# Layer 0 of a four-layer network: scans of 1024 tokens by channel halves, with the neighbouring images' stages in bands between them

## The chip, the cores and the metric

One core of one Trainium2 chip runs the whole kernel in one launch. The metric is the device time of a run in microseconds (us); a kernel's time is the median of its runs. The engines are named as in the profile: PE (TensorE), PEld (its weight loads), DVE (VectorE), ACT (ScalarE), POOL (GpSimd), SP (the queue that issues the DMAs).

## The reference, cut to what matters

The network has four layers over four images of 64 x 64 tokens and 128 features. Only layer 0 is touched. Its inside, cut:

```python
xz = x @ in_proj_w.T;  xh, z = split(xz, 2);  z = silu(z)      # 256 channels each
xc = silu(depthwise_conv3x3(xh) + conv_b)
xs = 4 directions of xc: by rows, by columns, and both reversed # K = 4
x_dbl = einsum('bkdl,kcd->bkcl', xs, x_proj_weight)             # 8 + 16 + 16 rows
delta = softplus(dt_projs(x_dbl[:8]) + bias)
A = -exp(A_logs)                                                # 16 states
# for each token:  h = exp(delta*A) * h + (delta*u) * B ;  y = sum_n h_n * C_n
y = ys + Ds * xs, summed over the four directions
y = layer_norm(y) * out_norm_w + out_norm_b;  y = y * z
return y @ out_proj_w.T                                         # then x + this (not shown)
# ... a group norm of x stands in front of it; layers 1 to 3 left out
```

The recurrence in h is what costs: 4 images x 4 directions x 4096 tokens x 256 channels x 16 states.

## The kernel before: the parts that are touched

A step is one direction `k` and one chunk `c` of 512 tokens, both channel halves.

```python
tmp = pool("l0tmp", 2);  ps = pool("l0ps", 2, space=PSUM);  psy = pool("l0psy", 1, space=PSUM)
for b in range(NB):
    # ... conv stage of image b, all of it: group norm, in_proj, 9 conv products a chunk,
    #     Silu into xc (whole image in SBUF), z to DRAM; all PE products in tag "m"

    def inputs(k, c):
        xd_ps = ps.tile([40, CH], F32, name="xd_ps", tag="m")
        # ... two products; ACT copies them to xd; rows 8:24 (B) go to DRAM
        for s in range(2):
            dp = ps.tile([P, CH], F32, name="dp", tag="m")
            nc.tensor.matmul(dp, lhsT=w_dt[...], rhs=xd[0:8, :], start=True, stop=True)
            nc.scalar.activation(delta[:, s, :], dp, AF.Softplus, bias=dt_b[:, k, s : s + 1])
        # ... POOL: du = delta * u

    for i, (k, c) in enumerate(steps):
        for g in range(4):                     # four states at a time
            Bb = tmp.tile([P, 4, CH], F32, name="Bb", bufs=3)     # B, broadcast by DMA
            h = big.tile([P, 2, CH, 4], F32, name="h", tag="h", bufs=2)
            for q in range(4):
                n = 4 * g + q
                dB = tmp.tile([P, 2, CH], F32, name="dB", bufs=3)
                nc.gpsimd.tensor_tensor(dB, du, Bb[:, q : q + 1, :].to_broadcast([P, 2, CH]), ALU.mult)
                for s in range(2):
                    dA = ps.tile([P, CH], F32, name="dA")
                    nc.scalar.activation(dA, delta[:, s, :], AF.Exp, scale=A_neg[:, k, s, n : n + 1])
                    nc.vector.tensor_tensor_scan(
                        h[:, s, :, q], dA, dB[:, s, :], state[:, s, n : n + 1], ALU.mult, ALU.add)
            # ... state saved; at g == 0: ready = inputs(next step)
            cr = ps.tile([P, CH], F32, name="cr", tag="m")        # C, spread for the products
            nc.tensor.matmul(cr, lhsT=sel[:, g, :], rhs=xd, start=True, stop=True)
            nc.vector.tensor_tensor(W, cr..., diag..., ALU.mult)
            for q in range(4):
                for e in range(2):
                    pt = ps.tile([P, 2, 2, P], F32, name="pt")
                    # ... four transposes of h into pt; ACT copies pt to hT (4 buffers)
                # ... four products yT += W * hT
        # ... y = yT (+ the earlier direction's y), stored; statistics of y at k == 2
    # ... norm/gate/out_proj stage of image b, all of it
```

## Time and profile before

| | before |
|---|---|
| median time | 10,989.8 us (4 runs, 10,984.5 to 11,016.0) |
| profiled span | 10,995.2 us, mean granted PE clock 0.910 of full |
| layer 0 ends near | 7,820 us |
| two steps (1024 tokens, both halves) | 98 to 107 us by direction |

The prediction below shows the slices, the stretches, the chain and the groups. Two more views are needed to compare with. The waits, as "engine line waited for: us in total, times, longest us":

```profile
POOL dB L242 <- DVE h L246: 1006.4, 829, 5.9
...
DVE h L246 <- POOL dB L242: 699.8, 10, 174.3
DVE h L246 <- ACT dA L245: 627.2, 924, 2.8
```

The 699.8 us are ten long waits, mostly the serial stages between images. Second, the stretch of the last direction of image 3 (start:end, length, busy and instructions of PE, PEld, DVE, ACT and POOL, then the granted clock, the DMA share and GB/s):

```profile
7312.26:7721.74 409.48, 356.35 (x2274) 174.00 (x2272) 344.00 (x352) 323.27 (x537) 306.85 (x156) 0.99 0.27 94
```

That is four times 1024 tokens, 102.4 us each, with PE at 87% and its clock at 0.99.

### The profile page before, as it was taken

To read this page: it belongs to the slowest core of one execution; us is meant where nothing else is said; L and a number is where in the kernel's file an instruction comes from. 1 tells how busy PE (TensorE), PEld (TensorE's weight loads), DVE (VectorE), ACT (ScalarE), POOL (GpSimd) and SP (SyncE) were. 2 spreads that over 40 slices of the span, in tenths; PEclk is the share of its full clock that TensorE was granted. 3 is DMA by queue.
4 is the path that set the end of the run, shared out by engine and by line. 5 is a ranking of instruction groups with operands and counts; after the bars stand their busy time and mean duration, and the time that the engine had idled before them with its cause. 6 is when DMAs were issued, how large, how long until landed. Compare 5 with 4: busy or idle time off the path is not lost.

```text
span 10995.2 us, 136237 instructions
## 1 busy us (share of the span) xinstructions
PE 9042.7 (82%) x48616; PEld 4817.3 (44%) x48616; DVE 7870.9 (72%) x11236; ACT 6496.6 (59%) x11794; POOL 5549.4 (50%) x3106
## 2 busy tenths in 40 slices
PE   8888887888888888888887888888797666576777
PEld 4433444443344344334444333444575334344555
DVE  2788887277888717788881778888445876877777
ACT  3778876377888727778871778887222102114555
POOL 2777877277788727778872777887200000000000
PEclk9999999889999988999998899999898667678999
DMA  2223322222233222223322222332300011010000
GB/s 71 86 98 105 108 101 92 74 86 94 101 110 106 86 79 87 95 99 110 105 91 69 97 95 102 107 108 95 106 16 22 20 31 31 0 31 7 9 9 9
DMA packets 375737, 811.01 MB, mean 74 GB/s; under 512 B 24546, under 2 KB 289506, under 8 KB 309266
## 3 DMA queue, kind: packets, MB, share of 16 engines
q1 hardware_dynamic: 372946, 799.82, 21.7%
q8 instruction: 385, 6.31, 0.2%
q14 instruction: 294, 2.41, 0.1%
q10 hardware_dynamic: 2112, 2.48, 0.1%
HBM read 680.58 MB, written 121.63 MB: 73 GB/s over the span
## 4 chain that ended last, share of the span: by engine, by line
PE 61%; DVE 21%; ACT 10%; issue 4%; DMA 2%; POOL 2%; ACTq 0%; DVEq 0%; SPq 0%; POOLq 0%
PE yT L277 15%; PE pt L269 14%; DVE h L246 10%; ACT hT L271 6%; PE cr L254 5%; PE cv L163 5%; PE pm L776 2%; PE xd_ps L193 2%; PE po L923 2%; ACT dA L245 2%; PE dp L201 2%; PE ps L891 1%; DVE W L256 1%; PE po L441 1%; PE pf L436 1%
## 5 line engine op out<-in xcount | busy, mean ns | idle before, releaser
L246 DVE TENSOR_TENSOR_SCAN h<-dA,state,dB 128x512 f32<-128x512 f32 x4096 | 5016.9, 1271 | 1398.9 <-POOL dB L242 699.8
L242 POOL TENSOR_TENSOR dB<-du,Bb 128x1024 f32<-128x1024 f32 x2048 | 4842.1, 2370 | 1267.6 <-DVE h L246 1006.4
L245 ACT ACTIVATE dA<-delta,A_neg 128x512 f32<-128x512 f32 x4096 | 2788.5, 696 | 527.8 <-DVE h L246 514.3
L269 PE MATMUL pt<-ident,h 128*128 128x128 f32 x16384 | 2667.0, 292 | 348.4 <-DVE h L246 348.1
L269 PEld LDWEIGHTS pt<-ident,h 128*128 128x128 f32 x16384 | 1838.6, 145 | 2000.1 <-issue 1280.2
L271 ACT COPY hT<-pt 128x512 f32<-128x512 f32 x4096 | 2252.5, 587 | 748.9 <-PE pt L269 737.8
L277 PE MATMUL yT<-hT,W 128*32 128x256 f32 x16384 | 2324.7, 403 | 355.5 <-ACT hT L271 353.2
L277 PEld LDWEIGHTS yT<-hT,W 128*32 128x32 f32 x16384 | 540.0, 109 | 1440.3 <-ACT hT L271 1019.9
L696 POOL COPY XG<-Xs 64x1 f32<-64x1 f32 x4 | 0.7, 180 | 1784.9 <-ACT Xs L667 1784.9
L204 POOL TENSOR_TENSOR du<-delta,xc 128x1024 f32<-128x1024 f32 x128 | 335.0, 2617 | 763.2 <-ACT delta L202 763.2
L254 PE MATMUL cr<-xd,sel 40*128 40x512 f32 x1024 | 624.6, 715 | 49.4 <-ACT delta L202 36.3
L256 DVE TENSOR_TENSOR W<-cr,diag 128x512 f32<-128x512 f32 x512 | 351.1, 686 | 395.4 <-PE cr L254 264.1
L163 PE MATMUL cv<-pad,taps 128*128 128x512 f32 x1152 | 496.2, 592 | 0.0
L883 POOL COPY vw<-pad 128x196 f32<-128x196 f32 x256 | 76.5, 350 | 702.6 <-PE pv L915 590.7
L193 PE MATMUL xd_ps<-xc,w_x 128*40 128x512 f32 x512 | 354.3, 817 | 93.4 <-DVE W L256 91.1
L776 PE MATMUL pm<-PT,Xs 64*128 64x512 f32 x512 | 380.3, 919 | 16.3 <-DVE pr L777 16.3
L163 PEld LDWEIGHTS cv<-pad,taps 128*128 128x128 f32 x1152 | 216.9, 189 | 278.0 <-issue 274.4
L170 ACT ACTIVATE xc<-cv,cols 128x512 f32<-128x512 f32 x64 | 44.0, 687 | 446.6 <-PE cv L163 446.6
L923 PE MATMUL po<-PT,V 98*128 98x256 f32 x1024 | 278.4, 394 | 35.6 <-DVE PT L919 35.6
L628 ACT COPY S<-pa 128x512 f32<-128x512 f32 x96 | 56.2, 585 | 420.6 <-PE pa L621 420.6
L201 PE MATMUL dp<-xd,w_dt 8*128 8x512 f32 x512 | 291.4, 653 | 6.1 <-ACT xd L195 6.1
L581 PE MATMUL in_pm<-in_mv,tok 128*128 128x32 f32 x48 | 14.1, 386 | 324.4 <-DVE in_mv L579 324.4
(268 smaller groups left out, 9455.2 us busy)
## 6 DMA issues: line engine op xcount, KB each, us to landing
Bb<-l_B SPq DMA_DIRECT2D x512, 1024.0 KB, 4.7
l_y<-y SPq DMA_DIRECT2D x128, 512.0 KB, 3.1
yr<-l_y SPq DMA_DIRECT2D x64, 512.0 KB, 4.8
l_z<-z SPq DMA_DIRECT2D x32, 512.0 KB, 2.9
zf<-l_z SPq DMA_DIRECT2D x32, 512.0 KB, 3.9
yr<-l_y SPq DMA_DIRECT2D x64, 256.0 KB, 4.9
yf<-l_y SPq DMA_DIRECT2D x32, 512.0 KB, 4.7
xt<-in_x SPq DMA_DIRECT2D x32, 256.0 KB, 3.0
```

The costliest lines, as they stand in the source:

```text
L163: nc.tensor.matmul(pm, lhsT=taps[:, s, t, :], rhs=pad[:, 8 * c + dy : 8 * c + dy + 8, dx : dx + 64], start=(t == 0), stop=(t == 8),)
L193: nc.tensor.matmul(xd_ps, lhsT=w_x[:, s, k, :], rhs=u[:, s], start=(s == 0), stop=(s == 1))
L201: nc.tensor.matmul(dp, lhsT=w_dt[:, k, s * P : (s + 1) * P], rhs=xd[0:8, :], start=True, stop=True)
L242: nc.gpsimd.tensor_tensor(dB, du, Bb[:, q : q + 1, :].to_broadcast([P, 2, CH]), ALU.mult)
L245: nc.scalar.activation(dA, delta[:, s, :], AF.Exp, scale=A_neg[:, k, s, n : n + 1])
L246: nc.vector.tensor_tensor_scan(h[:, s, :, q], dA, dB[:, s, :], state[:, s, n : n + 1], ALU.mult, ALU.add)
L254: nc.tensor.matmul(cr, lhsT=sel[:, g, :], rhs=xd, start=True, stop=True)
L269: nc.tensor.transpose(pt[:, r, s, :], h[:, s, t0 : t0 + 32, :].rearrange("p t n -> p (t n)"), sh.ident)
L271: nc.scalar.copy(hT, pt.rearrange("p r s d -> p r (s d)"))
L277: nc.tensor.matmul(yT[e][32 * jo : 32 * jo + 32, qo % 2, :], lhsT=W[:, 4 * q + j, :], rhs=hTs[j // 2][:, j % 2, :], start=((e, jo) not in ...
L776: nc.tensor.matmul(pm, lhsT=Xs[:, r, :], rhs=PT[:, 8 * g : 8 * g + 8, :], start=True, stop=True)
L923: nc.tensor.matmul(po[:, e], lhsT=V[:, half, :], rhs=PT[:, half].rearrange("p h q -> p (h q)"), start=(half == 0), stop=(half == 1),)
```

## The change

The intent: pay a scan's fixed cost (some 0.2 us) half as often, let PE make one `hT` per product in place of two, and hide the serial conv and norm stages of the neighbouring images between scans. A unit is now 1024 tokens of one channel half `s`; two units are a pair, the work of two old steps. `before(b+1)` and `after(b-1)` are generators whose pieces ("bands") are emitted at g == 2 and g == 1. The diff, cut to its core:

```diff
+    L = 2 * CH                                   # 1024 tokens; NQ = 8
-            # conv stage of the whole image (xn, xc in SBUF, tag "m")
+        def before(b):                           # 8 statistics pieces, then 8 x (pad piece, conv piece)
+            ...
+                    pm = ps.tile([P, CH], F32, name="cv", tag="pt")      # was tag "m"
+                    ...                                                   # 9 products
+                    xo = tmp.tile([P, CH], F32, name="xo", tag="t2", bufs=4)
+                    nc.scalar.activation(xo, pm, AF.Silu, bias=conv_b[:, s : s + 1])
+                    nc.sync.dma_start(scr(f"xr{b % 2}")[s, :, c * CH : (c + 1) * CH], xo)
+                    xw = tmp.tile([P, 64, 8], F32, name="xw", tag="t2", bufs=4)
+                    nc.vector.tensor_copy(xw, xo.rearrange("p (h w) -> p w h", w=64))
+                    nc.sync.dma_start(scr(f"xw{b % 2}")...[:, :, 8 * c : 8 * c + 8], xw)   # pieces of 32 B
+                    zp = ps.tile([P, CH], F32, name="zp", tag="pt")
+                    ...                                                   # Silu to z, z to DRAM
+        def after(b, st):                        # 8 norm/gate/out_proj bands, one POOL product each
+        def fetch(b, k, c):                      # u of the next pair, from xr or xw in DRAM
         def inputs(k, c, u):
-                    dp = ps.tile([P, CH], F32, name="dp", tag="m")        # 2 a step
+                    dp = ps.tile([P, CH], F32, name="dp", tag="pt")       # 4 a pair
-                Bb [P, 4, CH] bufs=3;  dB [P, 2, CH] bufs=3;  h [P, 2, CH, 4] bufs=2;  W, 2 bufs
+                Bb [P, 2, L] bufs=2;   dB [P, L] bufs=2;      h [P, L, 4] bufs=2;      W, 5 bufs
-                            dA = ps.tile([P, CH], F32, name="dA")         # 2 buffers, 2 banks
+                    dA = ps.tile([P, L], F32, name="dA")                  # 2 buffers, 4 banks
+                    nc.scalar.activation(dA, delta[:, s, :], AF.Exp, scale=A_neg[:, k, s, n : n + 1])
+                    nc.vector.tensor_tensor_scan(h[:, :, q], dA, dB, state[:, s, n : n + 1], ALU.mult, ALU.add)
-                    cr = ps.tile([P, CH], F32, name="cr", tag="m")
+                        cr = ps.tile([P, CH], F32, name="cr", tag="pt")   # 2 a group, at s == 0 only
+                if g == 1: next(post, None)      # a norm band
+                if g == 2: next(pre, None)       # a statistics, pad or conv piece
```

## The prediction

> **What bounds the kernel now.** I read the busy table and the 40 slices first, then stretches of one image, then the chain of waits, the groups, and the DMA list.
>
> The page's slices, from the span's start to its end (tenths busy):
> ```profile
> PE   8888887888888888888887888888797666576777
> DVE  2788887277888717788881778888445876877777
> ACT  3778876377888727778871778887222102114555
> POOL 2777877277788727778872777887200000000000
> ```
> The POOL line shows layer 0: four identical images, about 29 slices, the last layer-0 work ending near 7820 us of 10995 us. The rest is layers 1 to 3, which the change does not touch. Four dips of DVE and POOL are the serial stages between the scans. The stretches of image 0 (window, length, then busy and instruction count of PE, PEld, DVE, ACT, POOL, the granted clock, DMA share, GB/s):
> ```profile
> 188.00:1877.00 1689.00, 1472.23 (x8829) 687.12 (x8828) 1377.84 (x1265) 1345.25 (x2226) 1308.06 (x668) 0.95 0.28 99
> 1877.00:1962.00 85.00, 42.86 (x204) 37.09 (x204) 31.27 (x42) 10.54 (x18) 56.26 (x24) 0.67 0.46 137
> 1962.00:2136.00 174.00, 162.26 (x411) 75.91 (x410) 7.84 (x13) 34.56 (x56) 0.00 (x0) 0.95 0.10 33
> ```
> Scans take 1689 us, the norm/gate/out_proj stage 85 us, the next image's conv stage 174 us: a period of about 1957 us. In the scan stage four engines are 77 to 87% busy; none is saturated. The chain of waits over that stage says who leads:
> ```profile
> by line: PE yT L277 24.6%; PE pt L269 23.7%; DVE h L246 15.6%; ACT hT L271 9.6%; PE cr L254 8.0%; issue 4.0%; PE xd_ps L193 3.0%; ACT dA L245 2.9%; PE dp L201 2.9%; DVE W L256 1.8%; DVE y L300 0.7%; ACT delta L202 0.6%; ACT L202 0.5%; DMA B
> ```
> PE leads (transposes, products, cr, xd, dp), through the alternation transpose, copy, product. A timeline piece of PE in direction 0 (start, duration, idle before):
> ```profile
> 1120.02 0.64 PE L277 MATMUL yT<-hT,W 128*32 128x256 f32 x8
> 1120.59 1.09 PE L269 MATMUL pt<-ident,h 128*128 128x128 f32 x8
> 1121.97 0.41 PE L277 MATMUL yT<-hT,W 128*32 128x256 f32 x2 [0.29 <-ACT hT L271]
> ```
> Eight yT instructions take 0.64 us together though one alone is 403 ns: they run side by side. The groups give the unit costs:
> ```profile
> L246 DVE TENSOR_TENSOR_SCAN h<-dA,state,dB 128x512 f32<-128x512 f32 x4096 | 5016.9, 1271 | 1398.9 <-POOL dB L242 699.8
> L242 POOL TENSOR_TENSOR dB<-du,Bb 128x1024 f32<-128x1024 f32 x2048 | 4842.1, 2370 | 1267.6 <-DVE h L246 1006.4
> L245 ACT ACTIVATE dA<-delta,A_neg 128x512 f32<-128x512 f32 x4096 | 2788.5, 696 | 527.8 <-DVE h L246 514.3
> L271 ACT COPY hT<-pt 128x512 f32<-128x512 f32 x4096 | 2252.5, 587 | 748.9 <-PE pt L269 737.8
> ```
>
> [...]
>
> **The change, part by part.**
>
> *Scans.* A scan covers 1024 tokens of one channel half: 2048 scans in place of 4096. Each saves one fixed part: 2 x 1.262 - 0.19 gives about 2.31 us, so the sum of scan time falls by 2048 x 0.19 = 0.39 ms. Exponentials likewise: 256- and 512-column copies on ACT (372, 587 ns) give 0.84 ns a column, so 1024 columns cost about 1.12 us in place of 2 x 0.69. POOL's dB is the same, 2048 x 2.37 us.
>
> *PE.* A product is 128 columns wide, so it needs one hT, not two, and its four column groups run together: I estimate 0.35 us per half from the 0.57 us pitch of the 256-column ones, instead of two split halves of 0.56 us with waits. PE leaves the lead in the scans: per pair of scan units (1024 tokens, both halves, equal to two old steps of 52.7 us) PE has some 66 us.
>
> *The new loop.* dB has two buffers of one scan each (before: three of two scans). POOL may write dB n+2 only after scan n; the scan n+2 waits for it. The timeline shows 0.15 us from a scan's end to POOL's start and 0.08 us from POOL's end to a scan. A cycle of 2.31 + 0.15 + 2.37 + 0.08 = 4.91 us carries two scans, 2.455 us each: 32 scans take 78.6 us a pair. There is almost no slack in it, so what else stands on POOL or DVE mostly adds. POOL: two du (2.6 us) and six state copies (0.19): 6.3 us. DVE: eight W (0.69) 5.5, y additions 2.0, statistics 1.1: 8.6 us. If they hide behind each other entirely, DVE's and POOL's own sums of about 83 us bound; if they all add, 93.5. I choose 90. Softplus switches ACT's table away and back (1.283 us each) with copies between; that outlasts the two dA buffers: 4 us more. So 94 us a pair, against 105.4: 16 x 94 = 1504 us an image.
>
> *Bands, moved between scans.* The conv stage of image b+1 is 24 pieces in image b's 32 units. The built order puts the 18 convolution products of a band almost together on PE: 36 instructions of 0.43 us pitch, 15.5 us, and ACT holds two Silu pairs, nine copies and a table load before the next exponential. Against 4.7 us held in two dA buffers I get a DVE stall of 12.5 us a band: 100 us an image. The other pieces (xn, pad copies, statistics) cost about 30 us. The norm stage: one 2.35 us POOL product in place of three, four tensor_scalar[...], transposes, out_proj: about 9 us a band, 72 us. So 202 us an image is paid between scans, in place of 259 us of separate stages.
>
> *Added.* x is loaded and transposed twice; 64 more loads u of 1 MB; Bb traffic doubles to 1024 DMAs of 1 MB, one per two scans; 64 transposed stores xw of 8192 pieces of 32 B each; ACT table loads by the built order 321 in place of 277.
>
> *Sum.* Image 0's conv stage in bands, unhidden, with single-buffered xn and pad: 8 x 23 + 26 = 210. Image 0's scans with bands 1504 + 130; images 1 and 2 1504 + 202 each; image 3 1504 + 72; its norm stage 80. Together 6910 us against 7819: **-910 us, 10,080**; I predict **10,100 us**.
>
> **Rivals.**
> *The Bb load becomes the wait.* Its landing takes 4.7 us (median, 4.2 to 7.8). A Bb buffer now lasts two scans, about 4.9 us, and there are two: the load is just covered, and every y, u or B transfer put in front of it in the one queue is not. Before, a buffer lasted four POOL instructions of both halves and three were held, and the waits show nearly no DMA. The 32 B stores sharpen it: 512 B packets took 28 ns and 1 KB packets 47 ns in the trace (share times length over packets), so some 9 ns are fixed, and 512 packets per DMA engine would be 5 us by that line[...]; and Bb loads stand behind them. At 102 us a pair and 300 us of band stalls the same sum gives about 10,900 us.
> *Balanced engines reach their bound.* With DVE and POOL at 83 us a pair plus 5 for ACT and bands costing half, an image takes 1408 + 100 and the same sum gives about 9,400 us. For it: today DVE, ACT and POOL already run at 77 to 82% although PE leads. Against: two buffers everywhere.
> *PE stays the bound.* If the narrower products still cost 0.56 us, PE has 32 x (0.94 + 1.1) + 14 = 79 us a pair plus 10 for bands: close to the loop, some 3 us a pair more, 10,300 us.
>
> **Range and chances.** The central sum is 10,080; the pair's cost (88 to 101 us, 64 pairs) moves it by -380 to +450, the band stalls by -250 to +250. 9,550 to 10,700 should hold it 8 times in 10. Faster by over 2% needs under 10,773: 0.89. Within 2%: 0.08. Slower: 0.03.
>
> **What would show it.** Right: scans of about 2.31 us and exponentials of 1.12 us; DVE waiting for dB and POOL for h in turn at a pitch near 2.45 us; scan stages of an image at 1500 us plus bands; yT no longer leading the chain; gaps of 10 to 15 us on DVE at each conv band; layer 0 over near 6900 us and layers 1 to 3 as long as before. Wrong: POOL waiting for Bb DMAs, or the SP queue held by xw stores (rival one); PE yT still leading (rival three); or an image near 1500 us in all (rival two).

## More of the kernel before

A "bank" is here a PSUM buffer of 512 fp32 per partition. The kernel before holds eight of them in layer 0, two for each of four uses: `dA`, the transposes `pt`, everything else that PE makes (tag "m"), and the sums `yT`.

The scans (`DVE h`) wait for their two inputs, and never appreciably for `pt`.

## The result, and the profile after

| | before | after |
|---|---|---|
| median time, 4 runs each | 10,989.8 us | 11,966.4 us (11,955.1 to 11,969.7) |
| mean granted clock | 0.910 | 0.834 |
| mean scan | 1.271 us (512) | 2.342 us (1024) |
| layer 0 ends near | 7,820 us | 8,785 us |

The changed kernel is slower, by a ratio of 1.0882 (95% interval 1.0863 to 1.0900). A ratio is the mean time of one kernel's fast runs over the mean of the other's fast runs of the same rounds, so it is not quite the ratio of the medians quoted. The loss of some 970 us is all in layer 0.

The prediction's 1.262 us is the median scan of 512 tokens in the trace of before, and its 0.19 us of fixed time in a scan was my estimate. If a scan's time is a fixed part and a part that grows with its length, the two means of the table put the fixed part at 2 x 1.271 - 2.342 = 0.20 us.

The slices of DVE, ACT, POOL and the granted clock (in tenths), to be laid beside the prediction's:

```profile
DVE  2665556766555576655556666667735668777777
ACT  3665556655555566555556666666622111113555
POOL 2655556665555576655556666666700000000000
PEclk9888888887888888888888888888889776667999
```

The dips between images have gone, as intended. But DVE, ACT and POOL stand at 5 to 6 tenths where they stood at 7 to 8, and POOL's work, which marks layer 0, ends in the thirtieth slice of 299 us, at about 8.8 ms. Nothing is saturated. The chain of waits by line, and the groups:

```profile
PE pt L352 13%; DVE h L321 11%; POOL dB L318 9%; PE yT L361 8%; ACT hT L356 4%; DMA l_xw<-xw 3%; ACT dA L320 3%; PE pm L825 2%; DVE W L329 2%; PE po L972 2%; POOL du L266 1%; ACT L261 1%; PE ps L940 1%; PE cv L180 1%; ACT delta L261 1%
```

```profile
L321 DVE TENSOR_TENSOR_SCAN h<-dA,state,dB 128x1024 f32<-128x1024 f32 x2048 | 4751.9, 2342 | 2630.0 <-PE pt L352 2289.3
L318 POOL TENSOR_TENSOR dB<-du,Bb 128x1024 f32<-128x1024 f32 x2048 | 4835.1, 2370 | 2860.6 <-DVE h L321 2800.9
L352 PE MATMUL pt<-ident,h 128*128 128x128 f32 x16384 | 3194.0, 328 | 585.0 <-DVE W L329 288.7
```

The unit costs are as predicted (the exponential, not shown, has 1122 ns). The last field of the first row is new: the scans now wait 2289.3 us for the transposes, which have to free one of the two `h` buffers. The waits for the two buffers behind it:

```profile
DVE h L321 <- PE pt L352: 2289.3, 373, 16.2
...
PE pt L352 <- DVE W L329: 288.7, 237, 3.8
...
PEld pt L352 <- ACT z L196: 143.3, 24, 8.5
ACT z L196 <- DMA l_xw<-xw: 140.8, 25, 8.3
```

PE's transposes (and their weight loads) wait for DVE's W, which frees a buffer of cr, and for ACT's z, which itself waits for a DMA.

The pace can be read from the y stores: the time between the last store of one direction and of the next, over its four pairs. "Plain" is the last direction (k = 2), without bands (mean of four images); "conv" the pairs with a conv band (k = 3 and 0, images 0 to 2); "norm" those with two norm bands (k = 1, images 1 to 3).

| us a pair | plain | conv | norm |
|---|---|---|---|
| predicted | 94 | 106.5 | 112 |
| after | 114.1 | 148.8 | 136.0 |

The predicted 106.5 holds the conv band alone. A conv pair holds a pad piece too, and a norm pair of images 1 and 2 two statistics pieces; for all such pieces the prediction had 30 us an image.

**A pair without bands has one long stop, where its first unit turns to its second, and several short ones.** The timeline of DVE, ACT and PE there, in image 3's direction k = 0, which has no band either (start, duration, idle before and what ended it):

```profile
8065.01 4.58 DVE L321 TENSOR_TENSOR_SCAN h<-dA,state,dB 128x1024 f32<-128x1024 f32 x2
8074.35 4.59 DVE L321 TENSOR_TENSOR_SCAN h<-dA,state,dB 128x1024 f32<-128x1024 f32 x2 [3.45 <-PE pt L352]
8079.44 4.59 DVE L321 TENSOR_TENSOR_SCAN h<-dA,state,dB 128x1024 f32<-128x1024 f32 x2
8099.73 2.35 DVE L321 TENSOR_TENSOR_SCAN h<-dA,state,dB 128x1024 f32<-128x1024 f32 x1 [15.71 <-PE pt L352]
```

```profile
8082.95 1.28 ACT L261 ACT_TABLE_LOAD   x1
8084.25 1.26 ACT L261 ACTIVATE delta<-dp,cols 128x512 f32<-128x512 f32 x2
8085.53 1.28 ACT L320 ACT_TABLE_LOAD   x1
8086.83 1.12 ACT L320 ACTIVATE dA<-delta,A_neg 128x1024 f32<-128x1024 f32 x1
8087.96 1.28 ACT L261 ACT_TABLE_LOAD   x1
8089.26 1.26 ACT L261 ACTIVATE delta<-dp,cols 128x512 f32<-128x512 f32 x2
```

```profile
8084.99 3.78 PE L260 MATMUL dp<-xd,w_dt 8*128 8x512 f32 x4 [1.86 <-ACT delta L261]
8090.00 1.97 PE L352 MATMUL pt<-ident,h 128*128 128x128 f32 x8 [1.23 <-ACT delta L261]
```

The scan at 8099.73 needs the `h` of two groups before. That group's scans ended near 8069.6, but its transposes start at 8090.0. The four dp products (two instructions each) stand in front of them on PE and in the two buffers. A buffer comes free when ACT has made delta, and each two deltas stand behind a table load. A switch of tables costs 1.30 us here: the exponential begun at 8081.82 took 1.12 us, the load of 1.28 us starts at 8082.95 and the softplus at 8084.25. Then PE's transposes are slower at first (eight in 1.97 us with the clock granted at 0.50, later six in 0.88 with it at 1.00), and the scan starts 15.71 us late. The same wait also ended four short stops in the groups before it, of 1.70, 3.90, 4.17 and 3.45 us; there cr and W stand between two groups of transposes. The short stops weigh as much as the long one: of the 2289.3 us, 85 waits of over 10 us make 1,218 us, and 288 shorter ones 1,071 us.

**A conv band holds everything.** PE and ACT in one band:

```profile
3045.26 7.99 PE L180 MATMUL cv<-pad,taps 128*128 128x512 f32 x18 [2.98 <-ACT xo L188]
```

```profile
3053.29 0.69 ACT L188 ACTIVATE xo<-cv,cols 128x512 f32<-128x512 f32 x1 [7.60 <-PE cv L180]
3061.74 0.60 ACT L196 ACTIVATE z<-zp 128x512 f32<-128x512 f32 x1 [7.76 <-DMA l_xw<-xw]
```

The second conv sum (nine products, 18 instructions) waits for the first Silu, because both buffers are taken; the last z waits for a DMA; the transposes wait for z.

**The clock.** Slices of 2 us of the same plain stretch, columns as in the stretch of before:

```profile
8032.00:8034.00 2.00, 0.98 (x5) 0.30 (x4) 2.00 (x3) 0.90 (x1) 0.86 (x1) 1.00 0.62 229
8034.00:8036.00 2.00, 1.27 (x14) 0.65 (x13) 2.00 (x2) 0.86 (x3) 1.53 (x2) 0.56 0.94 353
8036.00:8038.00 2.00, 2.00 (x16) 1.30 (x14) 2.00 (x2) 1.83 (x3) 2.00 (x1) 0.50 0.35 73
...
8042.00:8044.00 2.00, 1.69 (x25) 1.05 (x24) 0.00 (x0) 1.65 (x3) 1.63 (x1) 1.00 0.07 29
```

PE had paused 1.02 us for DVE's W and 0.73 us for ACT. After that its clock is granted at 0.5 for some 7 us (0.50 in the slice from 8038, 0.73 in that from 8040); by 8042 it is back at full. Six transposes take 1.54 us from 8039.41 and 0.87 us from 8042.05. The kernel before had 0.99 in the last direction of image 3; this one has 0.85 there.

### The profile page after: what moved, and what is told of

It is laid out like the page before. It is cut to its first block, busy times and chain, and to the rows that moved or that the text cites.

```text
span 11965.9 us, 165895 instructions
## 1 busy us (share of the span) xinstructions
PE 9196.3 (77%) x65184; PEld 5251.5 (44%) x65184; DVE 7655.3 (64%) x9440; ACT 6240.3 (52%) x9822; POOL 5347.0 (45%) x3018
## 4 chain that ended last, share of the span: by engine, by line
PE 40%; DVE 22%; ACT 12%; POOL 11%; issue 11%; DMA 4%; SPq 0%; DVEq 0%; ACTq 0%; POOLq 0%
PE pt L352 13%; DVE h L321 11%; POOL dB L318 9%; PE yT L361 8%; ACT hT L356 4%; DMA l_xw<-xw 3%; ACT dA L320 3%; PE pm L825 2%; DVE W L329 2%; PE po L972 2%; POOL du L266 1%; ACT L261 1%; PE ps L940 1%; PE cv L180 1%; ACT delta L261 1%
## 5 line engine op out<-in xcount | busy, mean ns | idle before, releaser
L321 DVE TENSOR_TENSOR_SCAN h<-dA,state,dB 128x1024 f32<-128x1024 f32 x2048 | 4751.9, 2342 | 2630.0 <-PE pt L352 2289.3
L318 POOL TENSOR_TENSOR dB<-du,Bb 128x1024 f32<-128x1024 f32 x2048 | 4835.1, 2370 | 2860.6 <-DVE h L321 2800.9
L352 PE MATMUL pt<-ident,h 128*128 128x128 f32 x16384 | 3194.0, 328 | 585.0 <-DVE W L329 288.7
L320 ACT ACTIVATE dA<-delta,A_neg 128x1024 f32<-128x1024 f32 x2048 | 2296.4, 1122 | 1330.6 <-DVE h L321 1306.3
L352 PEld LDWEIGHTS pt<-ident,h 128*128 128x128 f32 x16384 | 2080.7, 163 | 1795.3 <-issue 942.1
L361 PE MATMUL yT<-hT,W 128*32 128x128 f32 x32768 | 1936.5, 313 | 704.7 <-ACT hT L356 701.8
L361 PEld LDWEIGHTS yT<-hT,W 128*32 128x32 f32 x32768 | 686.3, 115 | 1845.1 <-ACT hT L356 1406.8
L260 PE MATMUL dp<-xd,w_dt 8*128 8x512 f32 x512 | 380.1, 864 | 170.0 <-ACT delta L261 113.3
L191 DVE COPY xw<-xo 128x512 f32<-128x512 f32 x64 | 73.3, 1145 | 424.4 <-ACT xo L188 347.4
L266 POOL TENSOR_TENSOR du<-delta,u 128x1024 f32<-128x1024 f32 x128 | 302.3, 2362 | 89.0 <-ACT delta L261 84.1
L260 PEld LDWEIGHTS dp<-xd,w_dt 8*128 8x128 f32 x512 | 111.5, 247 | 385.1 <-ACT delta L261 205.8
```

The costliest lines, as they stand in the source:

```text
L260: nc.tensor.matmul(dp, lhsT=w_dt[:, k, s * P : (s + 1) * P], rhs=xd[0:8, es], start=True, stop=True)
L318: nc.gpsimd.tensor_tensor(dB, du, Bb[:, q % 2, :], ALU.mult)
L321: nc.vector.tensor_tensor_scan(h[:, :, q], dA, dB, state[:, s, n : n + 1], ALU.mult, ALU.add)
L352: nc.tensor.transpose(pt[:, j, :], h[:, t0 : t0 + 32, :].rearrange("p t n -> p (t n)"), sh.ident)
L361: nc.tensor.matmul(yT[e][32 * jo : 32 * jo + 32, qo % 4, :], lhsT=Ws[g][:, 4 * q + j, :], rhs=hT[:, j, :], start=((e, jo) not in started), ...
```

## The experiments

Theories at the outset. **Sharing (B; S in the second run's text):** the two PSUM buffers that serve the transposes and all else are the scarce thing. **Order (O):** PE runs its instructions in a fixed order, so transposes stand behind dp and cr whatever the buffers. **Tables (T):** softplus's table loads. **Depth (D):** two h buffers are too few. **Bands:** a band costs more between scans than in a stage. The Bb load, rival one of the prediction, fell with the trace: POOL waited 34.2 us for it in all.

Every run was compared with the kernel before in three rounds on the same chip (medians of before: 10,986 to 11,003 us). All outputs passed the comparison with the reference. That includes three that are wrong (two with Exp for Softplus, one with a wrong layout of xw): the tolerance on the network's output does not see such a difference in layer 0, nor does it tell a right softplus from a wrong one in 16 and 17.

### 1. The bands back as serial stages

```diff
-                if g == 1: next(post, None)
-                if g == 2: next(pre, None)
+            if i % per == per - 2 and b + 1 < NB:
+                for _ in before(b + 1): pass     # and after(b) drained at the image's end
```

> The changed kernel with its bands put back as two serial stages: the whole conv stage of the next image is drained in one go before the last pair of scan units, the norm stage of an image in one go after its last unit; everything else as changed. In the changed kernel a pair of units without a band takes about 115 us, with a conv band 145.5 us, with a norm band 125 to 140 us. Theory A (a conv band costs about 30 us between scans, more than the 23 us it costs alone): 3 images x (8 x 30 + 24 - 210) = about -160 us, 11,800 us; the plain pair stays at 115 us. Rival (the bands are mostly hidden, the loss is in the scan loop alone): serial stages come on top, +250 us or more, above 12,200 us.

Measured: 11,755.0 us, ratio 1.0695 to before; 211 us faster than the changed kernel. Theory A was right in direction and roughly in size; the pairs of k = 3 and 0, now without a band, take 116 to 118 us. With these buffers, interleaving costs more than it hides.

### 2. No table loads: Exp for Softplus

```diff
-                    nc.scalar.activation(delta[:, s, es], dp, AF.Softplus, bias=...)
+                    nc.scalar.activation(delta[:, s, es], dp, AF.Exp, bias=...)
```

> The changed kernel with Softplus replaced by Exp: a wrong result on purpose, the same instruction count, no ACT table load in the scan loop. Theory T (table switches make the 15.7 us stop of the scans once a pair): some 4 loads of 1.28 us a pair go, the stop shrinks to 10 us or less, 64 x 5.5 = -350 us, about 11,610 us. Theory S (the shared two PSUM buffers and the order on PE hold the transposes; the tables only lengthen it): -100 to -350 us, and the other stops of 2 to 4 us a group stay. If the tables were all of the stop: -900 us.

Measured: 11,812.9 us, ratio 1.0742; 153 us faster. Plain pairs 111.5 us in place of 114.1, the longest wait of a scan for pt 15.2 us in place of 16.2. Taken alone, the tables are a minor matter, at the lower end of theory S.

### 3 and 4. dA in SBUF, with shared and with own buffers

```diff
-                    dA = ps.tile([P, L], F32, name="dA")
+                    dA = tmp.tile([P, L], F32, name="dA")
```

and in the second also `tag="m"` in place of `tag="pt"` for every auxiliary product.

> Control for the next run: the changed kernel with dA in SBUF (two buffers of 128x1024) and nothing else; the auxiliary products still share the two PSUM buffers of the transposes. If the place of dA costs nothing, 11,966 us within 1% and scans of 2.34 us; if a scan from SBUF is slower or faster, it shows here, by 2048 x the difference.

> As the run with dA in SBUF, but the auxiliary products (xd, dp, cr, xh, cv, zp, statistics, op) get two PSUM buffers of their own, so that the transposes have their two alone, as in the kernel before. Theory S (the sharing is the cause): waits of the scan on the transposes mostly go, a plain pair falls from 115 to about 100 us and conv bands from 30 to about 20 us: some -1,200 us against the control, 10,800 us. Rival (PE executes in order, so the transposes stand behind dp and cr whatever buffers they have): less than -300 us.

Measured: 14,614.3 us (1.3295) and 13,742.9 us (1.2504). The control was not neutral. The scan's line of its trace (durations as min/median/max in ns):

```profile
L321 DVE TENSOR_TENSOR_SCAN h<-dA,state,dB x2048: 2293/2353/4562, 235.8 to 11331.3; 128x1024 f32<-128x1024 f32 x187
```

The median is that of the changed kernel, and so is that of POOL's dB (2357), but the means are 3220 and 3073 ns in place of 2342 and 2370: many instructions last nearly one instruction of the other engine longer. The longest scan took 4562 ns and the longest dB 4447 ns, each 2.1 to 2.2 us over its median; with dA in PSUM, in the changed kernel, the longest took 2381 and 2609 ns. What holds them is not shown; that the two engines hold each other up is my reading of these durations. The trace of before had shown the like: its 128x256 tensor_scalar on yf has a median of 407 ns and a maximum of 2573 ns, about one POOL product of 2.35 us more. In this kernel dA is better in PSUM: 11,966 us against 14,614. Between the two runs the only edit is the own buffers: -871 us. That speaks for sharing, but on a kernel with other waits.

### 5. Another program order

```diff
-  inputs(next) ahead of the transposes of group 0        +  behind them
-  cr and W of a group behind its scans                    +  ahead of them
```

> The changed kernel with two pieces of the program order moved and no buffer changed: the next unit's xd and dp products (and their softplus) are emitted behind the transposes of the first group in place of ahead of them, and cr and W of a group ahead of its scans in place of behind them. Theory O (what costs is the order on PE: the transposes stand behind dp, which waits for ACT's softplus, and behind cr, whose buffer waits for DVE's W after four scans): the stop of 15 us a pair and most of the 2 to 4 us a group go, a plain pair falls from 115 to about 100 us, 64 x 15 = -960 us, about 11,000 us, and the wait of the scans for the transposes falls from 2289 to under 1000 us. Theory B (the shared two buffers are the bottleneck in whatever order): they are handed out in another order but are as scarce, under -250 us.

Measured: 11,982.5 us, ratio 1.0894, no change; the scans wait 2224.3 us for pt. This does not refute theory O, because the edit could not test it. The trace shows that the build followed it: 504 of the 512 dp instructions stand directly ahead of the transposes of the second unit's group 0 in the changed kernel, and of its group 1 here. So the stop moved on by one group. For cr the edit changes nothing on PE: behind the scans of a group or ahead of them, it stands between the same two groups of transposes.

### 6. Half scans, own buffers

```diff
-                    dA = ps.tile([P, L], F32, name="dA")
-                    nc.scalar.activation(dA, delta[:, s, :], AF.Exp, scale=...)
-                    nc.vector.tensor_tensor_scan(h[:, :, q], dA, dB, state[...], ALU.mult, ALU.add)
+                    for e in range(2):
+                        es = slice(e * CH, (e + 1) * CH)
+                        dA = ps.tile([P, CH], F32, name="dA")
+                        nc.scalar.activation(dA, delta[:, s, es], AF.Exp, scale=...)
+                        first = h[:, CH - 1, q : q + 1] if e else state[...]
+                        nc.vector.tensor_tensor_scan(h[:, es, q], dA, dB[:, es], first, ALU.mult, ALU.add)
   ... and tag="m" in place of tag="pt" for every auxiliary product
```

> The changed kernel with the scans of a channel half cut back to two chained scans of 512 tokens, so that dA takes two PSUM buffers of one bank in place of two banks; the two banks that come free are given to the auxiliary products as buffers of their own. Units, bands, loads, stores and program order as changed. Cost by itself: 2048 x 0.19 = +390 us of DVE time and as much again hardly of ACT. Theory B (sharing of the buffers): in spite of that a pair falls to about 105 us, and bands to 20 us, some -800 us, 11,150 us. Theory O (order on PE): the transposes stand behind dp and cr still, the longer scans add: 12,000 to 12,350 us.

Measured: 10,895.5 us, ratio 0.9905 to before (0.9890 to 0.9920); 1,071 us faster than the changed kernel, in spite of the scan time put back, 2048 x (1.273 + 1.282 - 2.342) us or 0.44 ms. The scans' wait for pt falls from 2289.3 to 28.1 us. The order on PE changes too, without an edit that says so: see 9.

### 7. The kernel before, with sharing

```diff
-  tag="m"      +  tag="pt"        (every place)
```

> The kernel before with one thing of the changed one: all auxiliary products take the tag of the transposes, so that both share two PSUM buffers (two banks stay unused). Theory B: the waits of the changed kernel appear here, the scans wait for the transposes, and the time rises by 4% or more, above 11,400 us. Theory O: the order on PE is the same as before, within 1%, under 11,110 us.

Measured: 11,289.1 us, ratio 1.0263 (1.0248 to 1.0278): between the two expectations. The wait of the scans for the transposes appears (577.4 us), so sharing hurts the old kernel as well, but by a third of what it costs the new one. The old kernel's conv and norm stages are not between its scans.

### 8. Three buffers of h

```diff
-  h [P, L, 4], 2 buffers;  W, 5 buffers        +  h, bufs=3;  W, bufs=4
```

> The changed kernel with three buffers of h in place of two (and four of W in place of five, to fit SBUF). Theory D (depth: late transposes cost only because a scan may run just one group ahead of them): the third buffer lets the scans go on for 9.4 us more, the 15 us stop shrinks to 6 and the small ones vanish: a pair near 100 us, -800 us or more, 11,150 us. If PE's own stream of work with its waits is the bound, however far the scans run ahead: under -250 us.

Measured: 11,878.9 us, ratio 1.0797; 88 us faster. Theory D fails as the main cause: the wait for pt is still 2162.6 us. With one more group of depth the scans still end at the pace of PE's stream.

### 9. Half scans, shared buffers (the control of 6)

Experiment 6 without its change of tags.

> Control for the run with half scans and own buffers (10,896 us): the same two chained scans of 512 tokens and dA in two single banks, but the auxiliary products share the two buffers of the transposes as in the changed kernel; two banks stay unused. Theory B (sharing): the waits for the transposes come back, 11,900 to 12,400 us, that is the changed kernel's time plus part of the 390 us of added scan time. Rival (the gain came from dA's finer buffers, not from the own ones): 10,900 to 11,200 us.

Measured: 11,804.5 us, ratio 1.0736, just under the range that sharing gave. Own against shared buffers, with no other edit: **909 us**. The rival (that the finer dA buffers made the gain) accounts for the other 162 us, with the 436 us of added scan time already paid. The waits show it, first here, then with own buffers:

```profile
DVE h L324 <- PE pt L355: 1198.1, 230, 16.9
...
DVE h L324 <- PE pt L355: 28.1, 19, 2.7
```

The pace tells where the 909 us are:

| us a pair | plain | conv | norm |
|---|---|---|---|
| half scans, shared (9) | 112.7 | 145.9 | 131.7 |
| half scans, own (6) | 112.6 | 119.1 | 112.9 |

24 conv pairs x 26.8 and 12 norm pairs x 18.8 are some 870 us. So sharing is what the **bands** pay for; a plain pair does not gain from own buffers by themselves. There, in the last direction of image 0, the waits for pt go (29.2 us to 0), but those for dA grow (38.5 to 56.3 us), and ACT loads 26 tables in place of 16.

The 909 us need not be the wait for a buffer alone. In all kernels with the shared tag (the changed one, 2, 3, 5, 8, 9) every cr instruction stands between two groups of transposes and 504 of 512 dp instructions in one place. With own buffers the build spreads them (in 6 no place holds more than 104 of the dp). Own buffers thus bring another order on PE, and no run separates the two.

### 10. Own buffers, but cr shared

```diff
-                        cr = ps.tile([P, CH], F32, name="cr", tag="m")
+                        cr = ps.tile([P, CH], F32, name="cr", tag="pt")
```

> As the run with half scans and own buffers, but cr alone is put back into the two buffers of the transposes (xd, dp, conv, statistics and op keep their own). Lockstep theory (the 1,024 cr products are the costly sharers: cr gets a buffer only between two groups of transposes, W stands on DVE behind a scan that waits for those transposes, so a group's pitch becomes scan + W + eight transposes, 14.4 us in the trace of the changed kernel): most of the loss returns in the first units of each pair, about 4 us a group x 4 x 64 = +1,000 us, 11,900 us. Rival (dp with its softplus, and the conv bands, are the costly sharers): under +300 us, 11,000 to 11,200 us.

Measured: 11,044.7 us, ratio 1.0045; +149 us against 6. My lockstep theory (+1,000 us) is wrong; the rival's number is right, though dp and the bands are not told apart. Conv pairs take 124.7 us and norm pairs 119.1. The cr products alone (512, of two instructions each; the text above counts instructions) are cheap sharers. The trace has all of them between groups again, as in the shared form, while dp stays spread. It also has 689 table loads against 423 in 6, so the 149 us are not the price of sharing cr alone.

### 11. Own buffers, serial stages

Experiment 6 with the edit of 1.

> The run with half scans and own buffers with its bands put back as two serial stages, as in the first serial run. If the own buffers also make the interleaving worth while: a conv band costs some 12 us between scans there (pairs of 117 to 122 us against about 106), so 24 x 12 + 24 x 8 = 480 us of bands are replaced by 3 x 210 + 3 x 85 = 885 us of stages: +300 to +400 us, 11,250 us. Rival (the bands cost as much as the stages whatever the buffers): within 100 us of 10,896 us, or faster as in the shared case (-211 us).

Measured: 11,426.1 us, ratio 1.0394; +531 us against 6, more than expected. With shared buffers serial stages were 211 us faster, with own ones they are 531 us slower. The two pairs of runs differ in the scans (whole in the first, half in the second). The interleaving is worth while, but only once the bands do not take the transposes' buffers.

### 12. The transposed store without its 32 B pieces

```diff
-  scr(f"xw{b % 2}")[s].rearrange("p (w h) -> p w h", h=64)[:, :, 8*c : 8*c+8]     # 8192 pieces of 32 B
+  scr(f"xw{b % 2}")[s, :, c*CH : (c+1)*CH]                                        # wrong on purpose
```

> A wrong result on purpose: the run with half scans and own buffers with the transposed store xw written contiguously (512 elements a row in a piece, in place of 8192 pieces of 32 B). All else the same. If the 32 B store is what a conv band pays for (its landing of some 9 us holds the four shared row buffers, so z and the conv wait): 24 bands x 5 to 10 us, -120 to -240 us. If the store is hidden: within 50 us.

Measured: 10,858.1 us, ratio 0.9868; 37 us faster than 6, of 24 bands, at the edge of the noise (0.9846 to 0.9891 against 0.9890 to 0.9920 for 6). The store is nearly hidden with own buffers. It was not tried in the shared form, where the trace has z waiting 140.8 us for it, and where the 256 KB in 8192 pieces took 9.5 us from issue to landing (median) against 4.1 us for the same bytes of xr in long pieces.

### 13 and 18. Added PE work, to hold the clock

```diff
+  nc.tensor.matmul(wt, lhsT=..., rhs=..., start=True, stop=True)   # into an unused bank, read by nobody
```

First from constants, 40 a pair; then from the group's h, 32 a pair; both on the kernel of 9.

> The control with half scans and shared buffers (11,804 us) with added products that nobody reads: four 128x512 products into an unused PSUM bank per cr group and six after each dp, 40 a pair, so that TensorE pauses less; they add about 0.45 us each, 18 us of TensorE work a pair. Clock theory (after a pause of TensorE the clock is granted at 0.5 for 6 to 7 us, and the transposes that release the scans then take twice as long): the granted clock in pairs without a band rises from 0.85 to above 0.95 and a pair falls from 114 to about 105 us in spite of the added work, -500 us or more, under 11,300 us. Rival (the clock follows the waits and does not cause them): the added work comes on top, 11,800 to 12,300 us.

> The control with half scans and shared buffers (11,804 us) with four added products per group that nobody reads, made from that group's h so that the build cannot put them before its scans; 32 a pair, 0.45 us each, about 14 us of TensorE. Clock theory: the granted clock of pairs without a band rises from 0.85 above 0.95 and they fall from 114 below 108 us. Rival: the clock rises or not, the pairs get longer, 120 us or more, and the time 12,100 to 12,700 us.

Measured: 12,349.8 us (1.1237) and 13,343.4 us (1.2135). In the first the build ran the added products ahead of their place: the last direction of image 3 has 3180 PE instructions, as many as its control, so none of the added ones, and its pairs and clock are as before (109.8 us, 0.85). But in the last directions of images 0 to 2 some 83 added instructions a pair did run. The granted clock rose there to 0.94 to 0.96 (0.84 to 0.86 in the control), and yet the pairs took 121.9 to 123.7 us in place of 112.6 to 114.4: the higher clock did not make up for the work that raised it. In the second the clock there rose to 0.92 but PE was busy for 525 of 539 us (351 of 438 in the control): the added work itself became the bound. Its 128 products took 174 us more of PE, 1.36 us each, where I had expected 0.45. Both came out above even the rivals' ranges, and neither separates the clock from the waits. **How much of the loss the halved clock causes by itself stays open.**

### 14. Own buffers and no table loads

Experiment 6 with the edit of 2.

> The run with half scans and own buffers (10,896 us) with Softplus replaced by Exp (not the reference's formula), so that no table load stands in the scans. Table theory (the switches at the turn from one unit pair to the next make the 10 to 16 us stop there, the sharing only hid it): a pair without a band falls from 110 to about 100 us, -500 us, 10,400 us. If the loads count once and no more: 4 to 5 loads of 1.28 us a pair, -150 to -330 us, as in the shared form (-153 us).

Measured: 10,526.9 us, ratio 0.9578; 369 us faster than 6, between the two expectations; the same edit gave 153 us with shared buffers. The last direction of image 3, first of 6, then of this run:

```profile
7176.68:7615.30 438.62, 344.90 (x3151) 192.98 (x3150) 345.39 (x376) 329.78 (x539) 307.99 (x152) 0.82 0.47 166
```

```profile
6853.34:7246.01 392.67, 316.21 (x3150) 179.98 (x3150) 341.29 (x374) 300.17 (x517) 305.28 (x151) 0.90 0.53 185
```

Nearly the same instructions (ACT's fewer by the table loads) take 46 us less; DVE goes from 79% to 87% busy. Over the four images plain pairs fall from 112.6 to 100.5 us. In a plain pair the two causes seem to cover each other: own buffers alone 112.7 to 112.6, tables alone 114.1 to 111.5, both to 100.5. But the two axes start from different kernels (half and whole scans). Their plain pairs differ by only 1.4 us, yet in the last direction of image 3 the scans wait 89.1 us for pt with whole scans and only 22.9 us with half scans, buffers shared in both. Half scans with shared buffers and without table loads were not run, so that own buffers are needed for the 100.5 us is not shown.

The trace has 136 table loads here against 423 in 6, and 287 x 1.283 us is 368 us, the whole gain. That each load simply counts once does not follow: a plain pair lost some 6 loads, 8 us, and gained 12.1, while a norm pair gained nothing (112.9 to 113.5).

### 15. Own buffers and three buffers of h

> The run with half scans and own buffers (10,896 us) with three buffers of h (and four of W). Depth theory, now that the transposes have buffers of their own: a third group of scans rides over the stop at the turn of a pair, about 10 us of 110 a pair, -400 to -600 us, 10,400 us. If TensorE's stream is the bound there: within 100 us, as in the shared form (-88 us).

Measured: 10,804.9 us, ratio 0.9834; 91 us faster than 6. The expectation by depth (-400 us) is missed; the conv pairs gain (119.1 to 114.7), the plain ones do not (112.7).

### 16 and 17. The right softplus with one table switch

```diff
-                    nc.scalar.activation(delta[:, s, es], dp, AF.Softplus, bias=...)
+                    nc.scalar.activation(delta[:, s, es], dp, AF.Exp, bias=...)
+            nc.scalar.activation(delta, delta, AF.Ln, bias=1.0)      # once a pair, 128x2048
```

on the kernel of 6; then with three buffers of h as well.

> Half scans and own buffers (10,896 us), with the reference's softplus written as ln(1 + exp x): four Exp with the table that the scans use anyway, straight out of the dp buffers, then one Ln over the 128x2048 of a pair. ACT loads two tables a pair in place of four or five, and no dp buffer is held over a load. If the held dp buffers and the loads are the stop at the turn of a pair: near the run with Exp alone (10,527 us) plus 64 x (1.9 us of Ln and two loads, partly hidden), 10,560 to 10,720 us. If only the number of loads counts: 10,750 us or more.

> As the run with one Ln, with three buffers of h and four of W. The third buffer gave 91 us with own buffers and softplus, most of it in the pairs with conv bands. If it rides over the remaining Ln stop and the bands: -80 to -200 us against the run with one Ln. It is the candidate for a kernel that beats both, by 3% or more.

Measured: 10,664.7 us (0.9696) and **10,510.2 us (0.9564, 0.9545 to 0.9584)**. The first lands in its range; the third buffer adds 155 us. In the last kernel plain pairs take 99.8 us, conv pairs 113.5, norm pairs 115.6. It computes the reference's own formula and beats both kernels: 4.4% under the kernel before, and 12% under the changed one (0.9564 / 1.0882 = 0.879). Its trace has 264 table loads against 423 in 6, and the Ln takes 1.91 us.

## Why the prediction was wrong

**Right.** The 1024-token scan (2.31 us predicted, 2.342 measured), the exponential (1.12, 1.122), POOL's product (2.37), layers 1 to 3, the norm bands (9 us each predicted; two cost 136.0 - 114.1, so 10.9 each). That the norm bands came out near is in part luck: with own buffers two cost 0.3 us a pair (6), and with the tables gone too 13.0 (14), so here the shared buffers were part of their price, which the prediction did not count. The expected DVE stall at conv bands was seen, but not its size. Of the rivals, Bb as the wait fell with the trace. "PE stays the bound" came nearest, since the scans wait for PE, but not through the reason it gave: eight narrow yT products take 0.43 us at full clock (from 8097.64, granted 1.00).

**Wrong step one: "The new loop", 94 us a pair.** I took dB's two buffers between POOL and DVE for the loop, wrote "PE leaves the lead", and put softplus's table switches at 4 us because "that outlasts the two dA buffers". The real loop is: scans fill h, PE transposes it, h comes free; and PE stands in order behind dp, whose buffers are the transposes' own and come free behind table loads. The stop at the turn was 15.71 us, not 4, and a plain pair took 114.1 us. The rest fits the short stops of 2 to 5 us a group, where cr shares the same buffers. Taking the plain pair's loss for all 64 pairs, 64 x 20.1 is about 1,290 us. Experiments 2, 6 and 14 show that taking away the table loads alone (with whole scans) or giving own buffers alone (with half scans) leaves the pair above 111 us, and that it falls to 100.5 us with own buffers, half scans and no loads together.

**Wrong step two: "a DVE stall of 12.5 us a band".** A conv pair cost 148.8 - 114.1 = 34.7 us more than a plain one, up to 24 x 22 = 530 us more than said (its pad piece, for which the prediction had part of 30 us an image, is in it; against k = 3 and 0 of image 3, 117.7 us without a conv band, the band cost 31 us). I counted PE's 15.5 us against the two dA buffers. I did not count that the band's four products hand two buffers round through Silu and z, and that the transposes queue for the same two. Experiments 6 and 9 show it: with own buffers the band's excess over a plain pair is 6.5 us in place of 33. Some of that 6.5 is hidden behind the stop at the turn: without table loads (14) it is 16.2 us.

The two together, at most 1,820 us, are nearly all of the 1,886 us between the sum (10,080 us) and the result; the rest I did not trace.

**What was overlooked in both** is the count of PSUM banks. The diff has tag "pt" in every place of tag "m"; the prediction does not mention it. Where both causes are removed, my arithmetic comes within some 4 us: 94 us plus 32 x 0.213 us for cutting the scans in half is 100.8 us, and experiments 14 and 17 have 100.5 and 99.8. The 94 holds 4 us for table switches that 14 does not have, so 96.8 is the fair figure for it, and 17 has a third `h` buffer; that they agree to 1 us is in part luck. That the totals agree as well (10,080 + 436 against 10,510 us) I would not lean on, since conv bands cost some 14 us there and the stages differ.

**Open:** the clock's own share; how much of the 909 us is waiting for a buffer and how much the order on PE that a shared tag fixes; whether half scans without table loads would reach 100 us with shared buffers; and what the 32 B store costs in the shared form.

## What to carry to other kernels

Before enlarging a tile in PSUM, count the banks of all its neighbours (eight in both kernels here): what loses its own buffers is part of the change. Look for the slowest reader of a buffer that two streams share, and for what stands behind it: here a dp buffer was held until a softplus behind a table load of 1.28 us had read it, the transposes stood behind dp on PE until 8090.0, some 20 us after their scans had ended, and the next scan came 15.71 us late. In every shared kernel here the tag also fixed the order of those products on PE, so look at the built order on PE in the trace before you say what an edit changed. Try suspected causes together as well as singly: here removing either gave a plain pair 0 to 3 us and removing both (with half scans) gave 12, and bands that were a loss of 211 us with shared buffers were a gain of 531 us with own ones.
